# Attention in a hybrid block: one PSUM bank moved from the scores to the general pool, and half of the score products put behind the transposes of a query or key piece

## The chip, the cores and the metric

The kernel runs on one core of one Trainium2 chip. The metric is the time of one execution on the device in microseconds (us); lower is better. The kernel before the change took 1811.24 us, the median of three runs (1810.67 to 1813.12).

## What is computed

The reference is one hybrid block on x of shape 4 x 256 x 512 (four sequences of 256 positions, 512 channels), all in float32. Four residual steps follow each other, each on a layer norm of x: causal attention with 32 heads of 16 channels and an adapter of ten extra keys, a feed-forward with a selection of rows, a state space mixer (128 heads, by far the largest part), and the same feed-forward again. The change is in the attention:

```
q, k, v = split(x @ w_attn.T);  q, k = rope(q), rope(k)
scores  = q @ k.T / sqrt(16), causal
y       = softmax(scores) @ v
y      += gating * softmax(q @ ak.T / sqrt(512)) @ av     # ten adapter keys
out     = y @ w_proj.T
```

## The kernel before

The attention treats a sequence (b = 0 to 3) in eight units (u = 0 to 7) of four heads. This makes 32 iterations of the loop at line 705, numbered i = 8b + u. The stages of a unit are spread over several iterations, so that in iteration i the scores are of unit i, the transposes of the exponentials of unit i - 1, the product with the values of unit i - 2, and the gathering of unit i - 3. The inputs of later units and of the next sequence are made in the same iterations.

Everything that TensorE (PE) writes goes to PSUM, which has eight banks of 2 KB in each partition; every tile in question takes one bank. Three pools share them (lines 280 to 283): a_m with three banks, the general pool, whose tiles have the tag "m"; a_s with four banks for the scores (tag "sc"); and a_y with one bank for the product with the values. A tile that is asked for when all banks of its pool are taken gets the bank of an earlier tile, and its first writer waits until the readers of that earlier tile are done.

The order of PE's instructions is the order in which the code is written (manual_schedule at line 704). The instructions of the other engines are put in order by a planner that works with assumed costs. In one iteration PE does, in this order:

- **scores** (lines 475 to 510, a generator that yields twice). Eight products into four tiles: for c = 1 (the second 128 queries, against 256 keys) a pair of tiles of 2 x 256, then for c = 0 (the first 128 queries, against 128 keys) a pair of 2 x 128. Each tile takes two products (j = 0 and 1). Behind them VectorE (DVE) reads every tile twice at line 496 (it adds the mask, writes the sum to e and takes the maximum), eight reductions in all. Up to the first yield all this is issued; the second step issues the eight exponentials on ScalarE (ACT, line 505).
- **adapter_scores** (line 448, even iterations from 2 on): four products into "pa", copied to "sa" by ACT at line 456. Its second half transposes to "tra" later in the iteration, and ACT copies that to "as" at line 461.
- **pieces** (line 434): eight transposes into two tiles "trp" of a stack that POOL made, copied by ACT at line 444. They make a query or key piece for the scores of a later unit. Iterations 0 to 29 have them, 30 and 31 don't.
- the second step of **scores**, then the steps called "long" and "values": projections "pq" of the next sequence, output projections "po", the first products "pd" of the feed-forward (in iterations 30 and 31), all from groups of 512-wide or 288-wide products, and the adapter's product "pya", copied to "ya" by ACT at line 592.
- **weigh** (line 525): 16 products into "py", copied to "ys" by DVE at line 542.
- **turn** (line 512): twelve transposes into three tiles "ptr"; the first is copied to eT by ACT, the two others by DVE (line 522).
- **gathered** (line 545): two transposes of ys into "try", read by DVE at lines 553 and 554 (y).
- the rest of the adapter's scores, then the steps called "turn": the transposed norm "tr" (line 166; ACT and DVE copy it to axs at lines 107 and 108), "pt" (line 579) and "try" of line 605, which I call try2.

All of ptr, try, tra, trp, pa, tr, pt, pq, po, pd and pya are tiles of a_m. The pool a_s also holds the four projections of the first sequence before the loop (line 406).

In the loop the beginning of an iteration reads:

```
712  scoring = scores(b, u)
713  next(scoring)
...
721  if u % 2 == 0 and i > 0:
722      asides.append(adapter_scores(b, u // 2))
723      next(asides[-1])
724  if part:
725      next(part)
726  part = None
727  next(scoring)
728  step("long", i)
```

Of the kernel before, what the change touches and what calls it, by code (L numbers as in the profile page):

```python
# [79 lines left out]
def hybrid_kernel(  # L80
# [18 lines left out]
    a_s = keep.tile([P, 1], F32, name="a_s")  # L99
# [172 lines left out]
    def attention(later, region):  # L272
        with ExitStack() as es:
# [5 lines left out]
            p3 = pool("a3", 3)  # L279
            ps, ps_s, ps_y = (  # L280
                banks.enter_context(tc.tile_pool(name=name, bufs=bufs, space=PSUM))
                for name, bufs in (("a_m", 3), ("a_s", 4), ("a_y", 1))
            )

            acon = w1.tile([P, NCOL_ATTN - NCOL_KEEP], F32, name="acon")
# [181 lines left out]
            def begin(b):  # L467
                state[b] = {
                    "as": p1.tile([P, 2, NH, NA], F32, name="as"),
                    "y": p1.tile([P, 2, C], F32, name="y"),  # L470
                    "ya": p1.tile([P, 2, C], F32, name="ya", tag="ya"),
                    "yT": [p1.tile([P, KC, L], F32R, name=f"yT{j}") for j in range(2)],
                }

            def scores(b, u):

                qT, kT = turned_[b, u // 2]
                es_ = [p2.tile([P, 4, (c + 1) * P], F32, name=f"e{c}", tag=f"e{c}") for c in range(2)]
                made, tops = [], []
                for c in (1, 0):  # L480
                    n = (c + 1) * P

                    pair = [ps_s.tile([P, 2, n], F32, name="sc", tag="sc") for _ in range(2)]
                    for j in range(2):
                        blk = (u % 2) * 2 + j
                        for pr in range(2):
                            rows = slice(64 * pr, 64 * pr + 64)
                            nc.tensor.matmul(
                                pair[pr][:, j, :], qT[rows, blk, c * P : (c + 1) * P],
                                kT[rows, blk, :n], start=(j == 0), stop=(j == 1),  # L490
                            )
                    made += [(c, pr, sc) for pr, sc in enumerate(pair)]
                for c, pr, sc in made:
                    nm = p3.tile([P, 2], F32, name="nmx", tag="nmx", bufs=4)
                    for j in range(2):
                        nc.vector.tensor_tensor_reduce(  # L496
                            es_[c][:, 2 * j + pr, :].rearrange("p (k i) -> p k i", i=P),
                            sc[:, j, :].rearrange("p (k i) -> p k i", i=P), mask[:, 1 - c :, :],
                            -1.0, 3e38, ALU.add, ALU.min, nm[:, j : j + 1],
                        )  # L500
                    tops.append(nm)
                yield
                for (c, pr, sc), nm in zip(made, tops):
                    for j in range(2):
                        nc.scalar.activation(  # L505
                            es_[c][:, 2 * j + pr, :], es_[c][:, 2 * j + pr, :], AF.Exp, scale=-1.0,
                            bias=nm[:, j : j + 1],
                        )
                all_es[8 * b + u] = es_
                yield  # L510
# [120 lines left out]
            def fed(f, t):  # L631
                yield "turn", None
                xs = normed(f.norm, t)
                yield "long", max(0, B * 8 + t - 2)
                f.tile(t, xs, [ps.tile([P, FH], F32, name="pd", tag="m") for _ in range(2)])
# [41 lines left out]
            def moved(j, i):  # L677

                v = next(j, None)
                if v is None:  # L680
                    nexts.pop(j, None)
                else:
                    nexts[j] = v[0], i + 1 if v[1] is None else v[1]

            def step(stage, i):

                for j in [j for j, (s, r) in nexts.items() if s == stage and r <= i]:
                    moved(j, i)
# [15 lines left out]
            with tc.manual_schedule(engines={nc.tensor.engine}):  # L704
                for i in range(n):
                    b, u = divmod(i, 8)
                    if u == 0:
                        if i:
                            begin(b)
                        if b + 1 < B:  # L710
                            moved(prepared(b + 1), i)
                    scoring = scores(b, u)
                    next(scoring)
                    if i in FEEDS:
                        moved(fed(feed, FEEDS[i]), i - 1)
                    if i == 2:
                        nc.scalar.activation(a_s, a_s, AF.Exp)
                        nc.gpsimd.tensor_scalar(a_s, a_s, -1.0, None, ALU.mult)
                    if i == 3:
                        weights(wp_s, wproj, "ya", nc.gpsimd, p1)  # L720
                    if u % 2 == 0 and i > 0:
                        asides.append(adapter_scores(b, u // 2))
                        next(asides[-1])
                    if part:
                        next(part)
                    part = None
                    next(scoring)
                    step("long", i)
                    step("values", i)
                    if 2 <= i:  # L730
                        yss[i - 2] = weigh(*divmod(i - 2, 8), eTs.pop(i - 2))
                    if 1 <= i:
                        eTs[i - 1] = turn(all_es.pop(i - 1))
                    if 3 <= i:
                        gathered(*divmod(i - 3, 8), yss.pop(i - 3))
                    while asides:
                        next(asides.pop(0), 0)
                    step("turn", i)
                    if u == 7:
                        moved(adapted(b), i)  # L740
                    if 3 <= i:
                        if (i - 3) % 8 == 6:
                            moved(closed((i - 3) // 8, (0, 1, 2)), i)
                        if (i - 3) % 8 == 7:
                            moved(closed((i - 3) // 8, (3,)), i)

                    b, u = divmod(i + 3, 8)
                    if b < B:
                        part = pieces(b, u // 2, (i + 1) % 2)
                        next(part)  # L750
                    if i == 23:
                        inner.close()
                        feed = Feed("f", *(
                            later.enter_context(
                                tc.tile_pool(name=f"f{v}", bufs=v, side="right", reuse_waits="tile")
                            ) for v in (1, 2)
                        ))
                    if i in range(23, 27):
                        feed.weights(i - 23, nc.gpsimd)
                        feed.norm.stats(i - 23)  # L760
                    if i == 26:
                        feed.norm.root(0, 4)


                b = B - 1
                step("long", n)
                yss[n - 2] = weigh(b, 6, eTs.pop(n - 2))
                eTs[n - 1] = turn(all_es.pop(n - 1))
                gathered(b, 5, yss.pop(n - 3))
                step("turn", n)  # L770
                moved(fed(feed, 3), n - 1)
                step("turn", n)
                step("long", n + 1)
                step("values", n + 1)
                yss[n - 1] = weigh(b, 7, eTs.pop(n - 1))
                gathered(b, 6, yss.pop(n - 2))
                moved(closed(b, (0, 1, 2)), n)
                moved(fed(feed, 4), n)
                step("turn", n + 1)
                gathered(b, 7, yss.pop(n - 1))  # L780
                moved(closed(b, (3,)), n)
                step("long", n + 2)
                step("turn", n + 2)
                xs5 = normed(feed.norm, 5)
                assert not nexts, nexts
# [10 lines left out]
            with tc.tile_pool(name="f_c", bufs=5, space=PSUM, **freed) as ps_c:  # L796
# [22 lines left out]
                def products(t, j, cols=slice(0, FH)):  # L819
                    if (t, j) not in halves:  # L820
                        halves[t, j] = ps_c.tile([P, FH], F32, name="pd", tag="c")
                    feed.products(xss[t], j, halves[t, j], cols)
# [1010 lines left out]
    with ExitStack() as region:  # L1833
        mixer(*attention(later, region), later)
# [69 lines left out]
```

## Time and profile before

| What | Time |
|---|---|
| median of three runs | 1811.24 us |
| lowest and highest run | 1810.67, 1813.12 us |
| the profiled execution | 1812.82 us |
| its span, from the first to the last instruction | 1811.0 us |
| the stretch from 30 to 317 us, the attention loop | 287 us, PE busy 264.35, DVE 203.78, ACT 189.08, POOL 88.81 |
| from 317 to 400 us, the end of attention, the feed-forward and the start of the mixer | 83 us, PE busy 74.41, DVE 66.47 |
| from 400 us on, mostly the mixer | 1411 us, PE busy 1391.66 |
| TensorE clock granted, mean of the span | 0.994 |

The durations that the text works with come from the one profiled execution. All times inside it are counted from its first instruction. PE is TensorE with its products and transposes, PEld its loading of weights, DVE VectorE, ACT ScalarE, POOL GpSimd. A line such as "PE try L548 <- DVE eT L522: 3.2, 5, 1.1" says that PE, before instructions of line 548 that write the tile try, sat idle for 3.2 us in total, five times, at most 1.1 us, until instructions of DVE at line 522 that write eT had ended. In the timeline a row gives the start, the time taken, the engine, the line, the operation, the tiles (written <- read), the shapes and the number of instructions that were merged, and in brackets the idle time ahead of it and what ended it.

### The profile page before, as it was taken

What the parts mean: (1) busy time and instruction counts of PE and PEld (TensorE: products, weight loads), DVE (VectorE), ACT (ScalarE), POOL (GpSimd) and SP (SyncE); (2) the same over time, 40 slices, a digit from 0 to 9 for tenths busy, and PEclk for the clock granted to TensorE, in tenths of its full rate; (3) what the DMA queues carried; (4) which work ended last, traced back from release to release, by engine and by line L of the source; (5) the groups of instructions that cost most, each with busy time, mean ns of one, the idle gap of its engine ahead of it and who ended that gap; (6) DMA issues with size and microseconds to landing.
All of it is one profiled execution on the core that took longest, in us unless ns stands there. A gap on an engine that the chain in (4) does not pass through costs nothing.

```text
span 1811.0 us, 32937 instructions
## 1 busy us (share of the span) xinstructions
PE 1754.1 (97%) x12734; PEld 1425.0 (79%) x12734; DVE 1439.5 (79%) x2547; ACT 1268.4 (70%) x2289; POOL 250.9 (14%) x253
## 2 busy tenths in 40 slices
PE   8999988899999999999999999999999999999998
PEld 6777767778877888888888888888888888888877
DVE  6676677888998788878878797878787878887777
ACT  6666675487888667766866686768667866777754
POOL 6332230110110011011101111110111001101100
PEclk9999999999999999999999999999999999999999
DMA  4000000113243334423432343335323433343231
GB/s 151 1 1 1 23 15 26 43 59 106 94 134 125 105 94 135 134 76 103 162 109 93 94 146 99 100 94 170 99 93 104 154 105 94 111 140 112 85 98 57
DMA packets 134381, 169.51 MB, mean 94 GB/s; under 512 B 12240, under 2 KB 77520, under 8 KB 134224
## 3 DMA queue, kind: packets, MB, share of 16 engines
q1 hardware_dynamic: 125152, 134.37, 24.3%
q10 hardware_dynamic: 9072, 33.03, 4.8%
q8 instruction: 100, 1.64, 0.4%
q14 instruction: 57, 0.47, 0.1%
HBM read 131.71 MB, written 35.65 MB: 92 GB/s over the span
## 4 chain that ended last, share of the span: by engine, by line
PE 79%; DVE 10%; ACT 7%; issue 2%; POOL 1%; DMA 1%; SPq 0%; ACTq 0%; DVEq 0%; POOLq 0%
PE pp L115 14%; PE pp L117 13%; PE pp L116 13%; PE pyy L1244 8%; PE pog L115 6%; PE pog L116 6%; PE pog L117 6%; PE trx L1225 3%; PE ptr L521 1%; ACT e L505 1%; DVE acc L972 1%; PE pq L115 1%; PE pg L1162 1%; PE pq L116 1%; DVE eT L522 1%
## 5 line engine op out<-in xcount | busy, mean ns | idle before, releaser
L115 PE MATMUL pp<-mx,w 128*128 128x512 f32 x1144 | 459.3, 401 | 0.0
L117 PE MATMUL pp<-mx,w 128*128 128x512 f32 x1144 | 446.7, 391 | 0.0
L116 PE MATMUL pp<-mx,w 128*128 128x512 f32 x1144 | 446.1, 390 | 0.0
L1277 POOL TENSOR_TENSOR sq<-sq,x 128x1024 f32<-128x1024 f32 x54 | 132.1, 2446 | 1177.8 <-ACT x L1276 1177.8
L117 PEld LDWEIGHTS pp<-mx,w 128*128 128x128 f32 x1144 | 214.8, 188 | 46.2
L115 PEld LDWEIGHTS pp<-mx,w 128*128 128x128 f32 x1144 | 214.8, 188 | 44.6
L972 DVE SCALAR_TENSOR_TENSOR acc<-pp,cw_s,acc 128x1012 f32<-128x1012 f32 (+2 forms) x192 | 244.6, 1274 | 4.3
L116 PEld LDWEIGHTS pp<-mx,w 128*128 128x128 f32 x1144 | 215.2, 188 | 40.4
L1218 DVE TENSOR_TENSOR em<-em,gm 128x1280 f32<-128x1280 f32 x128 | 189.5, 1489 | 72.1 <-ACT em L1213 72.1
L115 PE MATMUL pog<-wo,gh 128*128 128x512 f32 x512 | 200.7, 392 | 1.9 <-DVE x L1373 1.9
L117 PE MATMUL pog<-wo,gh 128*128 128x512 f32 x512 | 199.7, 390 | 0.9 <-DVE gh L1356 0.9
L116 PE MATMUL pog<-wo,gh 128*128 128x512 f32 x512 | 199.4, 389 | 0.0
L1228 DVE TENSOR_TENSOR xd<-trx,dt_t 128x512 f32<-128x512 f32 x128 | 82.4, 686 | 141.4 <-PE trx L1225 141.4
L1144 ACT ACT_TABLE_LOAD x63 | 80.8, 1283 | 138.8 <-DVE acc L972 138.7
L1435 ACT ACTIVATE gt<-pp 128x1024 f32<-128x1024 f32 x64 | 65.6, 1025 | 145.2 <-PE pp L117 145.2
L1244 PEld LDWEIGHTS pyy<-em,xd 64*64 64x64 f32 x4096 | 130.2, 133 | 44.2 <-issue 17.3
L1205 ACT ACTIVATE em<-r,end_t 128x128 f32<-128x128 f32 x512 | 163.0, 389 | 0.8
L1244 PE MATMUL pyy<-em,xd 64*64 64x256 f32 (+3 forms) x4096 | 157.8, 300 | 3.1 <-DVE em L1218 2.9
L115 PEld LDWEIGHTS pog<-wo,gh 128*128 128x128 f32 x512 | 96.1, 188 | 24.7 <-issue 2.7
L117 PEld LDWEIGHTS pog<-wo,gh 128*128 128x128 f32 x512 | 96.1, 188 | 22.2 <-DVE gh L1356 2.1
L116 PEld LDWEIGHTS pog<-wo,gh 128*128 128x128 f32 x512 | 96.1, 188 | 19.4
L505 ACT ACTIVATE e<-e,nmx 128x256 f32<-128x256 f32 (+1 forms) x256 | 96.6, 450 | 19.9 <-DVE nmx L496 19.3
(323 smaller groups left out, 3131.8 us busy)
## 6 DMA issues: line engine op xcount, KB each, us to landing
wr<-in_win_dram SPq DMA_DIRECT2D x144, 256.0 KB, 2.8
r<-cumd SPq DMA_DIRECT2D x256, 128.0 KB, 2.9
spill<-gb ACTq DMA_DIRECT2D x63, 512.0 KB, 2.8
gr<-spill SPq DMA_DIRECT2D x120, 256.0 KB, 3.5
wor<-in_wout_dram SPq DMA_DIRECT2D x64, 256.0 KB, 4.5
out_dram<-x SPq DMA_DIRECT2D x7, 256.0 KB, 2.6
x<-in_x_dram SPq DMA_DIRECT2D x1, 1536.0 KB, 8.8
gr<-spill SPq DMA_DIRECT2D x8, 192.0 KB, 2.5
```

The costliest lines, as they stand in the source:

```text
L115: nc.tensor.matmul(o, lh, rh, start=(first and k == 0), stop=False)
L116: nc.tensor.matmul(o, lh, rl, start=False, stop=False)
L117: nc.tensor.matmul(o, ll, rh, start=False, stop=(last and k == n - 1))
L505: nc.scalar.activation(es_[c][:, 2 * j + pr, :], es_[c][:, 2 * j + pr, :], AF.Exp, scale=-1.0, bias=nm[:, j : j + 1],)
L972: nc.vector.scalar_tensor_tensor(av[:, :, d:], pv[:, :, : L - d], cw_s[:, ch, tap : tap + 1], av[:, :, d:], ALU.mult, ALU.add,)
L1144: nc.scalar.activation(pair(x2).rearrange("p k u i -> p u k i"), acc.rearrange("p (u k i) -> p u k i", u=2, i=Q), AF.Silu,)
L1205: nc.scalar.activation(piece(e, j, c, 2 - c, 2), rv[:, j, 2:, :], AF.Exp, bias=end_t[:, 2 * j + c, h : h + 1],)
L1218: nc.vector.tensor_tensor(e, e, gm, ALU.mult)
L1228: nc.vector.tensor_tensor(xd[:, hs, :].rearrange("p c (h d) -> p c h d", h=2), tr.rearrange("p c (h d) -> p c h d", h=2), dt_t[:, hs, 2 * ...
L1244: nc.tensor.matmul(py[d, u, j * L + c * Q : (j + 1) * L].rearrange("p (k i) -> p k i", i=Q), xd[us, 4 * j + c, d], piece(es2[hh], j, c)[us ...
L1277: (nc.gpsimd if n < NB - 2 else nc.vector).tensor_tensor(sqs[g], sqs[g], x2, ALU.add)
L1435: nc.scalar.activation(gts[i], pp, AF.Silu)
```

## The change

Three things change, all in the attention.

1. The pool a_m gets four banks instead of three, a_s three instead of four.
2. The generator of the scores yields three times instead of twice. Its first step now issues the four products of the second queries (c = 1) and their four reductions, its second step the four products of the first queries (c = 0) and their four reductions, and its third step the eight exponentials. The functions products and reduced hold the same instructions as before.
3. The loop calls the generator once more, behind the transposes of the piece. So on PE the adapter's four products and the eight transposes now stand between the products of the second and those of the first queries.

No instruction is added or taken away. The full diff:

```
-                for name, bufs in (("a_m", 3), ("a_s", 4), ("a_y", 1))
+                for name, bufs in (("a_m", 4), ("a_s", 3), ("a_y", 1))
...
                 made, tops = [], []
-                for c in (1, 0):
+
+                def products(c):
                     n = (c + 1) * P
-
                     pair = [ps_s.tile([P, 2, n], F32, name="sc", tag="sc") for _ in range(2)]
                     for j in range(2):
                         blk = (u % 2) * 2 + j
...
-                    made += [(c, pr, sc) for pr, sc in enumerate(pair)]
-                for c, pr, sc in made:
+                    for pr, sc in enumerate(pair):
+                        made.append((c, pr))
+                        reduced(c, pr, sc)
+
+                def reduced(c, pr, sc):
                     nm = p3.tile([P, 2], F32, name="nmx", tag="nmx", bufs=4)
                     for j in range(2):
                         nc.vector.tensor_tensor_reduce(
...
                     tops.append(nm)
-                yield
-                for (c, pr, sc), nm in zip(made, tops):
+
+                for c in (1, 0):
+                    products(c)
+                    yield
+                for (c, pr), nm in zip(made, tops):
                     for j in range(2):
                         nc.scalar.activation(
                             es_[c][:, 2 * j + pr, :], es_[c][:, 2 * j + pr, :], AF.Exp, scale=-1.0,
...
                     if part:
                         next(part)
                     part = None
+                    next(scoring)
                     next(scoring)
                     step("long", i)
                     step("values", i)
```

More of the change, by code (lines that the diff above doesn't have):

```diff
@@ L281, in attention @@
                 banks.enter_context(tc.tile_pool(name=name, bufs=bufs, space=PSUM))
-                for name, bufs in (("a_m", 3), ("a_s", 4), ("a_y", 1))
+                for name, bufs in (("a_m", 4), ("a_s", 3), ("a_y", 1))
             )
@@ L479, in scores, with products @@
                 made, tops = [], []
-                for c in (1, 0):
+                def products(c):
                     n = (c + 1) * P
@@ L491, in scores, with reduced @@
                             )
-                    made += [(c, pr, sc) for pr, sc in enumerate(pair)]
-                for c, pr, sc in made:
+                    for pr, sc in enumerate(pair):
+                        made.append((c, pr))
+                        reduced(c, pr, sc)
+                def reduced(c, pr, sc):
                     nm = p3.tile([P, 2], F32, name="nmx", tag="nmx", bufs=4)
@@ L501, in scores @@
                     tops.append(nm)
-                yield
-                for (c, pr, sc), nm in zip(made, tops):
+                for c in (1, 0):
+                    products(c)
+                    yield
+                for (c, pr), nm in zip(made, tops):
                     for j in range(2):
@@ L726, in attention @@
                     part = None
+                    next(scoring)
                     next(scoring)
```

## The prediction

> **What bounds the kernel now.** I read the page first: TensorE (PE) is busy 97% of the span and has 79% of the chain that ended last. Then the busy times by stage: the change touches only the attention loop, from about 30 to 300 us. Then the waits of PE in 24 to 320 us, and the timeline around them.
>
> ```profile
> PE 1754.1 (97%) x12734; PEld 1425.0 (79%) x12734; DVE 1439.5 (79%) x2547; ACT 1268.4 (70%) x2289; POOL 250.9 (14%) x253
> ...
> PEclk9999999999999999999999999999999999999999
> ```
> ```profile
> 107.00:166.00 59.00, 57.27 (x464) 44.53 (x460) 42.67 (x175) 37.99 (x94) 18.00 (x33) 1.00 0.01 2
> 166.00:175.00 9.00, 7.38 (x75) 5.74 (x74) 7.19 (x31) 6.55 (x16) 2.87 (x5) 1.00 0.00 0
> ...
> 231.00:252.00 21.00, 16.37 (x157) 12.95 (x158) 14.53 (x58) 17.12 (x39) 8.91 (x13) 0.93 0.04 13
> 252.00:283.00 31.00, 27.76 (x234) 20.87 (x233) 23.38 (x99) 21.26 (x54) 3.31 (x8) 0.93 0.01 2
> ```
> The columns are the stretch, its length, then busy time of PE, PEld, DVE, ACT and POOL, and the granted clock. Where an iteration holds a 512-wide product (107 to 166) PE is all but full. Where it holds none (166 to 175, and 231 to 283) PE is idle a tenth to a fifth of the time and waits for evictions:
>
> ```profile
> PE try L548 <- DVE eT L522: 3.2, 5, 1.1
> PE ptr L521 <- ACT ya L592: 2.2, 1, 2.2
> ...
> PE pq L115 <- ACT sa L456: 0.9, 2, 0.4
> ...
> PE tr L166 <- DVE eT L522: 0.8, 2, 0.4
> ```
> "try" does not read eT: it waits for a bank of the general pool a_m that the copy to eT still reads. Likewise ptr on ya, pq on sa, tr on eT. These are the waits a fourth bank can end.
>
> **What the change adds.** Scores of one iteration fill four tiles: two wide ones (second queries) and two narrow ones (first queries). With four banks in a_s nothing waits. With three, the second narrow tile reuses the bank of the first wide one, and has to wait until DVE has done both reductions of that tile. Iteration 13 shows whether the transposes cover this (PE, then DVE):
>
> ```profile
> 141.56 0.68 PE L488 MATMUL sc<-pc,pc 64*128 64x256 f32 x8
> 142.17 0.89 PE L442 MATMUL trp<-con,st 128*128 128x128 f32 x8
> 142.90 0.50 PE L115 MATMUL pq<-wv,axs 128*128 128x512 f32 x1
> ```
> ```profile
> 142.21 0.42 DVE L496 CUSTOM_DVE_ANT_0 e<-sc,acon 128x256 f32<-128x256 f32 x1 [0.28 <-PE sc L488]
> ...
> 142.56 0.28 DVE L554 TENSOR_TENSOR y<-try,ry 128x128 f32<-128x128 f32 x1
> 142.76 0.41 DVE L496 CUSTOM_DVE_ANT_0 e<-sc,acon 128x256 f32<-128x256 f32 x1
> ```
> They do not. The four wide products take 0.34 us (start of the fifth product less start of the first, in the trace), the eight transposes 0.73 (142.17 to 142.90), so after the change PE wants that bank at about 141.56 + 0.34 + 0.73 + 0.07 = 142.70. The second reduction ends at 142.76 + 0.41 = 143.17. A semaphore takes about 0.06 (an eT copy that ends at 141.22 lets tra start at 141.28), and three narrow products behind it 0.20 (three times 0.068, from four in 0.27). So pq starts at second end + 0.26 = 143.43 and not at 142.90: **0.53 us lost**, all on PE's path, since 12 products queue behind in order and the rotation on DVE, the copies on ACT and the next transposes wait for them. In even iterations four adapter products (0.53) stand between as well: in iteration 4 the second reduction ends 1.61 after the first score product, so 1.87 is wanted, and pq starts at 1.93 anyway. No wait there, only one more change from transposes to 64-row products. No row shows this change alone; between nothing and the 0.17 us that PEld idles ahead of score weights now, I take 0.07, what trp costs more behind adapter products than behind scores (0.80 against 0.73).
>
> The same sum for every iteration, with the end of the second reduction and the present start of what follows on PE, both counted from the first score product, and the loss (end + 0.26 - start):
> 0: 2.36, 2.05, 0.57. 1: 1.46, 1.47, 0.25. 3: 2.02, 1.83, 0.45. 5: 1.73, 1.45, 0.54. 7, 13, 15, 21, 23: 1.61, 1.34, 0.53 each. 9 and 17: 2.02, 1.74, 0.54 each. 10: 2.13, 1.95, 0.44. 11 and 19: 1.84, 1.34, 0.76 each. 18: 1.90, 2.07, 0.09. 25: 1.42, 1.59, 0.09. 27: 1.84, 1.80, 0.30. 29: 2.36, 2.18, 0.44. Sum 8.4.
> The nine even ones without a wait (2, 4, 6, 12, 14, 20, 22, 26, 28): 0.07 each, 0.6.
> 8, 16, 24: 0.52, 1.06, 1.10, where DVE's softmax sums of the adapter come first. I count nothing: there ptr is followed by a wait for DVE (1.0 us at 171.57) that begins only when the last reduction ends, and the late ptr hides in it.
> 30 and 31 have no transposes between (the pieces are used up): 2.35 against 1.15, 1.46; 2.10 against 0.61, 1.75. Behind them ptr, tr and try now wait 0.77 + 0.38 and 0.75 for banks, which the fourth bank frees, so 0.3 and 1.0 remain: 1.3.
> **Cost 8.4 + 0.6 + 1.3 = 10.3 us.** The narrow reductions themselves do not come late: DVE works on the wide ones until 2.30 after the start, and their tiles are there by about 2.1. No DMA and nothing on POOL is moved; reductions pass only copies that are ACT's.
>
> **What the change removes.** Waits of PE for a bank of a_m, from its timeline. Left out are those that end in data (POOL's stacks, y, axs) and those already in the starts above or used up at 30 and 31. First the wait, then what I count:
> First iterations, 41.90 to 44.02 (0.62, 0.39, 0.21) and 52.03 (0.68): 1.9, all, since the bank then comes from a tile copied long before. 60.41: 0.2, all.
> tr at 116.19 and 183.76 (0.41 each), try2 at 125.10 and 192.79 (0.38), tr at 274.32 (0.38): 2.0, all.
> pq or po behind sa at 135.62, 203.31, 267.92 (0.44, 0.43, 0.53): 0.31, 0.31 and 0.5, together 1.1, since the scores' bank is next at the first two (pq 2.07 after the first score product and not 2.38).
> The groups behind 8, 16 and 24 (1.4, 1.6, 1.4): 1.1, as the reductions set the pace and the late ptr eats the rest.
> try at 234.52: 1.06, all; its data, ys, was there at 232.99.
> ptr at 249.24 (2.19): 0.9. Its second tile gets a bank that was free at 244.5, the third still waits for ya behind eight exponentials; eight transposes took 1.76 there, half of it moves into the wait.
> try, tra and try2 at 256.56 to 264.95 (1.0): 0.7. pt at 306.18 and 307.45 (1.0): 0.7.
> **Gain 9.6 of 15.1 listed.** The lower end is a third of the list, 5.0 (each wait moves on to the next tile, as at ptr); the upper all of it. I take each by the data behind it, as said.
>
> **Sum.** +10.3 - 9.6 = +0.7 us. The profiled execution took 1812.82 us (span 1811.0 and 1.8 around it), so 1813.5 for it; it lies 1.6 above the median of the runs, 1811.24, and against that the forecast is **1811.9**.
>
> **The clock.** The rows show it at half in short stretches: granted 0.93 over 231 to 252 and again over 252 to 283. At 259.50 the eight transposes take 1.15 to the next product instead of 0.73, and the py group 1.44 instead of 0.79; with ptr's 1.91 for 1.53 that is about 1.4 us a stretch. It followed waits of only 0.35, 0.16 and 0.53. So a stretch more or fewer is 1.4 either way, and I take none. The Trainium skill, TensorE: Matmul & The Clock Gate, "What's actually happening", halves the clock after an idle window of about 3.4 us; by it the new waits, of half a microsecond to two, would never slow PE, and the sum would stay. This trace has it sooner. The same page, Part 4, says that transposes don't count as busy as products do, which fits 256 to 260, nearly all transposes.
>
> **Rivals.**
> The fourth bank wins. All 15.1 come back and 30 and 31 hide whole: 15.1 - 9.0 = 6.1 faster, **1805.1**. For it: the last eight iterations have few wide products, and PE waits most there. Against it: in 8 and 16 DVE's reductions, not a bank, hold the next step.
> The scores' wait is not hidden in 8, 16, 24, 30 and 31. This is the slower side: PE comes late to ptr there, and DVE waits for PE instead. Price 2.7 for the three and 1.9 for the two: +5.3, **1816.5**. It decides from the point where ptr's second tile comes after DVE would start to copy it: in iteration 16 that is 4.04 (ptr, now 2.98, plus 1.06) + 1.1 = 5.14 after the first score product against 4.79, so it is near.
> The fourth bank doesn't do what it says: tiles wait for the next slow copy, only a third is gained: 10.3 - 5.0, again +5.3, 1816.5. Against it: the waits at 116, 183 and 234 have their data ready.
> If DVE takes the two wide reductions without y between them (0.20), the new waits shrink by 0.2 in some 15 iterations, 3.0 less; that is inside the range.
>
> **Chances.** Forecast 0.44, fourth bank wins 0.24, wait not hidden 0.24, bank of no use 0.08. This kernel can be told from no change by about 0.2%, 3.6 us. The forecast's own range is that of no change, 1807.6 to 1814.9; the others are one faster, two slower: 0.24, 0.44, 0.32. The bounds of the terms (cost 6 to 15, gain 5 to 15) and two stretches of clock reach from 1804.5 to 1819.5.
>
> **What would show it.** Right: sc of four and four, the second four starting about 0.5 us after trp in odd iterations, waiting for DVE L496; trp starting 0.27 sooner after the wide scores; no wait of tr, try or pq on eT or sa at iterations 10, 11, 12. Wrong: no wait ahead of the narrow scores, or ptr waiting there for L496; and a changed number of half-clock stretches would add what the sum leaves out.

## The result, and the profile after

| | median | lowest to highest | runs |
|---|---|---|---|
| before | 1811.47 us | 1810.67 to 1813.12 | 4 |
| after | 1820.62 us | 1819.47 to 1821.81 | 4 |

The ratio is 1.0044, with a 95% interval of 1.0031 to 1.0057: the change makes the kernel slower, by 5.6 to 10.3 us. The forecast was 1811.9 us and no difference, with a range of its own from 1807.6 to 1814.9 us. The profiled execution of the changed kernel took 1819.51 us, with a span of 1817.7 us.

The page of the changed kernel, busy times and granted clock:

```profile
PE 1765.8 (97%) x12734; PEld 1438.1 (79%) x12734; DVE 1439.4 (79%) x2547; ACT 1269.1 (70%) x2289; POOL 250.4 (14%) x253
...
PEclk8999999999999999999999999999999999999999
```

PE has the same 12,734 instructions and is busy 11.7 us longer. An instruction also counts as busy while it runs at half clock or stands behind another, so this alone names no cause. The same four stretches as before (stretch, its length, busy PE, PEld, DVE, ACT, POOL, granted clock):

```profile
107.00:166.00 59.00, 56.82 (x441) 45.08 (x439) 40.37 (x171) 37.16 (x92) 16.72 (x32) 1.00 0.01 2
166.00:175.00 9.00, 8.48 (x87) 6.65 (x85) 7.60 (x30) 6.44 (x17) 4.22 (x6) 1.00 0.00 0
231.00:252.00 21.00, 19.61 (x166) 15.00 (x158) 17.16 (x65) 15.60 (x35) 12.21 (x17) 0.92 0.11 30
252.00:283.00 31.00, 27.27 (x233) 21.34 (x233) 22.82 (x98) 24.33 (x60) 4.17 (x11) 0.94 0.00 1
```

Where the iteration holds 512-wide products (107 to 166), PE now starts 441 instructions in 59 us, where it started 464 before. (The same times hold slightly earlier work in the changed kernel, whose iteration 13 begins at 144.14 and not at 141.56, so these rows give an impression and no sum.) The view of what PE waited for, 24 to 330 us of the changed kernel (total us, times, longest):

```profile
PE sc L488 <- DVE nmx L499: 12.5, 22, 1.9
...
PE ptr L527 <- DVE eT L528: 0.8, 1, 0.8
PE try L554 <- DVE eT L528: 0.8, 1, 0.8
...
PE tra L460 <- ACT eT L528: 0.4, 1, 0.4
...
PE tr L166 <- ACT paT L589: 0.2, 1, 0.2
PE try L611 <- ACT eT L528: 0.2, 1, 0.2
```

The waits on eT, sa, ya and as that stood in the view of before (13.9 us in all) are down to 2.2 (the four lines here that end in eT). The fourth bank does its work. In their place stands one line that was not there: the products of the scores wait 22 times for DVE's reductions, 12.5 us. The following table shows that this line understates them. It splits the time from the first score product of iteration 0 to the start of the last pya product, 32 iterations, into two sums of start times on PE: from the first score product of each iteration to the first product behind scores, adapter products and the piece's transposes (the score piece), and all the rest. The last three kernels are experiments told below.

| kernel | score piece | rest | together |
|---|---|---|---|
| before | 59.6 | 224.3 | 283.9 |
| after | 81.0 (+21.4) | 209.4 (-14.9) | 290.5 (+6.5) |
| split alone | 67.6 (+8.0) | 222.3 (-2.0) | 289.9 (+5.9) |
| four general banks shared with py, scores unsplit | 52.4 (-7.2) | 212.6 (-11.7) | 265.0 (-19.0) |
| the same, scores split | 61.3 (+1.7) | 212.1 (-12.2) | 273.4 (-10.5) |

From before to after the rest gives back 14.9 us, and the score piece takes 21.4. Outside this part the spans differ by 0.2 us. Iteration 13 of the changed kernel shows the piece, PE first, then DVE:

```profile
144.14 0.50 PE L488 MATMUL sc<-pc,pc 64*128 64x256 f32 x4
144.58 0.89 PE L442 MATMUL trp<-con,st 128*128 128x128 f32 x8
145.39 0.32 PE L488 MATMUL sc<-pc,pc 64*128 64x128 f32 x1
145.91 0.41 PE L488 MATMUL sc<-pc,pc 64*128 64x128 f32 x3 [0.19 <-DVE nmx L499]
146.25 0.50 PE L115 MATMUL pq<-wv,axs 128*128 128x512 f32 x1
```
```profile
144.79 0.42 DVE L499 CUSTOM_DVE_ANT_0 e<-sc,acon 128x256 f32<-128x256 f32 x1
145.14 0.08 DVE L499 DVE_READ_ACCUMULATOR2_ANT nmx<- 128x1 f32 x1
145.14 0.29 DVE L560 TENSOR_TENSOR y<-try,ry 128x128 f32<-128x128 f32 x1
145.34 0.41 DVE L499 CUSTOM_DVE_ANT_0 e<-sc,acon 128x256 f32<-128x256 f32 x1
145.68 0.08 DVE L499 DVE_READ_ACCUMULATOR2_ANT nmx<- 128x1 f32 x1
```

The second narrow product waits, as forecast, for both reductions of the first wide tile; the read of their accumulator, which the forecast did not have, ends at 145.76. pq then starts 2.10 us after the first score product; before it was 1.34. That is 0.77 (with the unrounded starts) and not 0.53. The bracket says 0.19: it counts idle time only from the modelled end of the product ahead, 145.39 + 0.32. But nothing keeps the second narrow product from starting with the first: in the split kernel with four score banks it starts 0.003 or 0.004 us after it in all 32 iterations. Here it starts 0.52 us after it.

Read in this way, the products wait in 31 of the 32 iterations (all but iteration 2), from 0.15 to 2.16 us and 21.7 us in all, where the view shows 22 waits and 12.5 us. In iteration 4, where the forecast saw no wait, the second narrow product starts 0.15 us after the first, and the row has no bracket; the four take 0.56 us and not the 0.44 that they take where nothing holds them:

```profile
71.70 0.56 PE L488 MATMUL sc<-pc,pc 64*128 64x128 f32 x4
72.19 0.50 PE L115 MATMUL pq<-wq,axs 128*128 128x512 f32 x1
```

### The profile page after: what moved, and what is told of

It reads as the page before. It is cut to its first block, busy times and chain, and to the rows that moved or that the text cites. A ratio compares the mean times of both kernels' runs of the same rounds, so it can differ in the third digit from the quotient of the medians.

```text
span 1817.7 us, 32954 instructions
## 1 busy us (share of the span) xinstructions
PE 1765.8 (97%) x12734; PEld 1438.1 (79%) x12734; DVE 1439.4 (79%) x2547; ACT 1269.1 (70%) x2289; POOL 250.4 (14%) x253
## 4 chain that ended last, share of the span: by engine, by line
PE 78%; DVE 11%; ACT 6%; issue 2%; POOL 1%; DMA 1%; ACTq 0%; SPq 0%; DVEq 0%; POOLq 0%
PE pp L115 12%; PE pp L117 12%; PE pp L116 12%; PE pyy L1251 7%; PE pog L115 6%; PE pog L116 6%; PE pog L117 6%; PE trx L1232 3%; PE ptr L527 2%; DVE acc L979 2%; ACT em L1212 1%; PE pq L115 1%; DVE em L1225 1%; PE sc L488 1%; PE pq L116 1%
## 5 line engine op out<-in xcount | busy, mean ns | idle before, releaser
L919 DVE TENSOR_TENSOR w<-wr,w 128x512 fp32r<-128x512 f32 x138 | 99.7, 727 | 4.4 <-ACT w L916 4.4
```

Of the source, the lines that this page charges most:

```text
L919: nc.vector.tensor_tensor(w[1], r, w[0].bitcast(F32), ALU.subtract)
```

## The experiments

The theory at the start of the experiments: the split has a price of its own, the narrow products' wait comes on top, and the fourth bank gives back about what the list of waits says. The rival: the fourth bank does nothing, and the wait is the whole cost.

**Split alone** (three general banks, four for scores; the generator and the loop as in the change):

```diff
-                for name, bufs in (("a_m", 4), ("a_s", 3), ("a_y", 1))
+                for name, bufs in (("a_m", 3), ("a_s", 4), ("a_y", 1))
```


> The split of the scores with the banks as before (three general, four for scores). Theory: the loss has three terms, the wait for the scores' third bank (12.5 us of PE idle in the changed kernel), a fixed price of taking the four wide and four narrow products apart (about 0.2 us an iteration, 6 us in all: 0.61 us for eight together; apart, the four wide ones take 0.44, the change to 64-row products 0.09 more, the narrow ones 0.27), and more half-clock stretches. Here the first is gone and the 15 us of waits for the general pool remain: some 6 us over before, about 1817.5, and no wait of PE at L488 on the reductions. Rival, that the split is nearly free and the wait is all (the prediction had 0.07 us in nine iterations): within 2 us of before, 1811 to 1813.

Measured: 1820.19 us, ratio to before 1.0043 (1.0026 to 1.0060). The split alone, without any wait for a scores' bank, costs about as much as the whole change. The median is above what either side expected, but the interval (4.7 to 10.9 us) holds the theory's 6. Iterations 13 and 6 in its timeline of PE:

```profile
148.10 0.51 PE L488 MATMUL sc<-pc,pc 64*128 64x256 f32 x4
148.64 0.84 PE L442 MATMUL trp<-con,st 128*128 128x128 f32 x8
149.41 0.44 PE L488 MATMUL sc<-pc,pc 64*128 64x128 f32 x4
149.78 0.50 PE L115 MATMUL pq<-wv,axs 128*128 128x512 f32 x1
```
```profile
88.39 0.50 PE L488 MATMUL sc<-pc,pc 64*128 64x256 f32 x4
88.82 0.70 PE L452 MATMUL pa<-pc,akbd 128*80 128x256 f32 x4
89.36 0.46 PE L442 MATMUL trp<-con,st 128*128 128x128 f32 x4
90.07 0.51 PE L442 MATMUL trp<-con,st 128*128 128x128 f32 x4 [0.25 <-ACT sa L456]
90.51 0.44 PE L488 MATMUL sc<-pc,pc 64*128 64x128 f32 x4
90.88 0.50 PE L115 MATMUL pq<-wv,axs 128*128 128x512 f32 x1
```

Nothing is idle in iteration 13 by the brackets, and pq still comes 1.68 after the first score product, 0.34 later than before. Four wide products alone take 0.43 (iteration 6) or 0.54 us until the next product starts, four narrow ones 0.37 until pq, together 0.80 to 0.91; all eight in one go took 0.61. In iteration 6 the second transposes also wait 0.25 for a bank; such waits of trp, ended by ACT at sa, come seven times in this kernel (1.9 us). The view of before has none for trp, and neither has that of the split kernel with four general banks below, so they belong to the split with three.

**Banks alone** (four and three, the scores not split; the second step of the generator follows the first at once):

```diff
-                for name, bufs in (("a_m", 3), ("a_s", 4), ("a_y", 1))
+                for name, bufs in (("a_m", 4), ("a_s", 3), ("a_y", 1))
```


> Four general banks and three for scores, with the narrow products directly behind the wide ones as before. Theory: the wait for the third bank is then no longer covered by transposes and adapter products; the second reduction ends about 1.6 to 2.4 us after the first product, the narrow ones want the bank at 0.4: some 1.4 us in each of 32 iterations, 45 us, less about 15 us of waits for the general pool and less what hides in light iterations: 1835 to 1845. Rival, that the wait hides behind other waits: no slower than the changed kernel, 1820.

Measured: 1867.27 us, ratio 1.0301 (1.0281 to 1.0321). Its waits of PE:

```profile
PE sc L488 <- DVE nmx L499: 43.3, 29, 2.2
```

The theory expected 45 us of this wait and 1835 to 1845 us in all. The view's 43.3 fits only in appearance: by the starts, the second narrow products wait 1.1 to 2.4 us in each iteration, 55.0 us together. The score piece is 51.0 us longer than before (110.6 us), and the rest, which was to give back some 15, is 3.5 longer too. From the first score product to the last pya product 78.5 us run at half clock, 17.1 in before; what share of the time that makes was not tried. So the split is what makes three score banks bearable at all: it leaves 21.7 of 55 us of waiting, at a price.

**py in the general pool, scores as before** (no bank of its own for py; four and four):

```diff
-                for name, bufs in (("a_m", 3), ("a_s", 4), ("a_y", 1))
+                for name, bufs in (("a_m", 4), ("a_s", 4))
...
-                py = ps_y.tile([P, L], F32, name="py", tag="py")
+                py = ps.tile([P, L], F32, name="py", tag="m")
```


> The kernel before with four banks in the general pool and four for the scores; the product py has no bank of its own and takes one of the general pool. Scores as before, not split. Theory: the waits for the general pool (15 us listed before, 2.4 left in the changed kernel) go with no price: 1798 to 1803. Rival, that such a wait only moves to the next tile or engine (the prediction counted 9.6 of 15.1 and py takes a bank): 1805 to 1811.

Measured: 1796.24 us, ratio 0.9919 (0.9900 to 0.9939). A fourth general bank is worth 11 to 18 us if it is taken from py and not from the scores; the median lies a little under the theory's 1798 to 1803. This is the fastest of all kernels here, faster than before and after.

**Narrow scores first** (the changed kernel, with the first queries' products ahead of the transposes and the second queries' behind):

```diff
-                for c in (1, 0):
+                for c in (0, 1):
```


> The changed kernel with the pairs in the other order: the narrow products (first queries) ahead of the transposes, the wide ones behind. The bank is then released by two narrow reductions (0.28 us each instead of 0.42). Theory: the release comes 0.3 to 0.4 us sooner, the 12.5 us of waiting fall to about 4, the fixed price stays: 1810 to 1814. Rival, that the half-clock stretches and not the wait make the loss: 1818 to 1821 as the changed kernel.

Measured: 1813.3 us, ratio 1.0003 (0.9993 to 1.0014). The time is as expected, the wait isn't: 9.0 us in 15 waits. By the starts of the products the wait is 17.5 us, where the changed kernel has 21.7. That the tile with the short reductions is freed sooner does shorten the waits, by 4 us, but the time fell by 7. The mean granted clock of the twelve runs is 0.9933, that of the changed kernel's four 0.9898, so the rival (the half-clock stretches) may have a part in it. The time therefore doesn't confirm the reason.

**Split with shared py**, to settle whether the split's price hangs on the banks:

```diff
-                for name, bufs in (("a_m", 4), ("a_s", 3), ("a_y", 1))
+                for name, bufs in (("a_m", 4), ("a_s", 4))
...
-                py = ps_y.tile([P, L], F32, name="py", tag="py")
+                py = ps.tile([P, L], F32, name="py", tag="m")
```


> Here the general pool has four banks (the py tiles among them), the scores have four, and the scores are split as in the changed kernel, so no score product should wait for a bank. The theory says that the split has a fixed price, about 8 us, which the split alone showed with no wait for a scores' bank, and that it is paid whatever the pools are: 1796.2 us of the unsplit kernel with the same banks plus 8 = about 1804 us (1801 to 1807). The rival says that the price of the split alone came from the split work meeting three general banks (its trace shows 1.9 us of trp waits on sa that were not there before): then it goes with four general banks, and the time is 1796 to 1799 us.

Measured: 1804.51 us, ratio 0.9960 (0.9948 to 0.9973); the rival, 1796 to 1799, falls. Iteration 13 of the unsplit kernel with these banks, then of this one:

```profile
134.03 0.68 PE L488 MATMUL sc<-pc,pc 64*128 64x256 f32 x8
134.64 0.89 PE L442 MATMUL trp<-con,st 128*128 128x128 f32 x8
135.36 0.46 PE L115 MATMUL pq<-wv,axs 128*128 128x512 f32 x1
```
```profile
140.08 0.50 PE L488 MATMUL sc<-pc,pc 64*128 64x256 f32 x4
140.52 0.88 PE L442 MATMUL trp<-con,st 128*128 128x128 f32 x8
141.32 0.44 PE L488 MATMUL sc<-pc,pc 64*128 64x128 f32 x4
141.69 0.50 PE L115 MATMUL pq<-wv,axs 128*128 128x512 f32 x1
```

1.33 us became 1.61, with no wait in either. The same difference, 0.26 to 0.32, stands in 17 of the 21 iterations from 3 to 23; the other four (8, 10, 16, 18) lie between -0.14 and 0.22. These 17 make 4.9 of the 9.0 us by which the two score pieces of the table differ; iterations 25 and 26 make 2.0 more.

**Three banks shared by the general pool and py**, one bank idle (against the kernel with shared py, scores unsplit):

```diff
-                for name, bufs in (("a_m", 4), ("a_s", 4))
+                for name, bufs in (("a_m", 3), ("a_s", 4))
```


> Here py shares the general pool as in the fast kernel, but that pool has three banks and one bank lies idle; scores unsplit, four banks. The theory says that the fourth general bank is what gained there, and that giving py a place in a pool of three takes a bank away from the others now and then: no faster than before, 1812 to 1822 us. The rival says that it was py that gained, since it no longer waits for its one bank: then this kernel is about as fast as the one with four shared banks, 1796 to 1802 us.

Measured: 1819.92 us, ratio 1.0040 (1.0027 to 1.0052). So it is the fourth bank that gains, not py's sharing. The waits of PE are many and small:

```profile
PE ptr L521 <- ACT eT L522: 2.0, 6, 0.4
PE ptr L521 <- DVE ys L542: 1.9, 5, 0.5
...
PE tra L460 <- ACT eT L522: 1.5, 2, 0.8
```

ptr reads neither eT nor ys; it waits for their banks.

**Second products and exponentials behind the step "long"** (against the changed kernel):

```diff
+                    step("long", i)
                     next(scoring)
                     next(scoring)
-                    step("long", i)
```


> The changed kernel with the second four products, and the exponentials, behind the step called long instead of ahead of it. The theory says that the products then find their bank free (the 12.5 us of waits fall to 2 or less), while the fixed price of the split, about 8 us, and the gain of the fourth general bank, about 15 us, stay: 1820 - 11 = about 1808 us (1804 to 1812). The rival says that the later reductions and exponentials are late for the transposes of the next iteration, so that the wait comes back there as a wait for the exponentials: 1815 us or more.

Measured: 1812.03 us, ratio 1.0002 (0.9993 to 1.0012), the upper end of the theory's range. Both sides were partly right:

```profile
PE tra L460 <- ACT eT L528: 4.6, 8, 0.8
PE sc L488 <- DVE nmx L499: 3.4, 5, 1.0
...
PE pa L452 <- ACT eT L528: 2.0, 3, 1.5
PE try L611 <- ACT eT L528: 1.5, 3, 0.7
```

The wait for the scores' banks falls from 12.5 to 3.4 (by the starts of the products from 21.7 to 4.5), and the waits for ACT's copies to eT, 0.6 in the changed kernel, come to 8.1 in the lines shown. That ACT copies late since its exponentials now come behind "long" is argued from the order, not tried.

**Five general banks** (py among them, three for scores, narrow first):

```diff
-                for name, bufs in (("a_m", 4), ("a_s", 3), ("a_y", 1))
+                for name, bufs in (("a_m", 5), ("a_s", 3))
...
-                for c in (1, 0):
+                for c in (0, 1):
...
-                py = ps_y.tile([P, L], F32, name="py", tag="py")
+                py = ps.tile([P, L], F32, name="py", tag="m")
```


> Scores split with the narrow ones first, three banks for them, and five for the general pool with py among them. The theory says that a fifth general bank finds nothing left to gain, that the split costs its 8 us, and that the wait for a scores' bank stays at about 9 us: 1796 + 8 + 9 = 1813, less what such waits let the other engines catch up, so 1807 to 1814 us. The rival says that general banks are still short at four: then 1798 to 1804 us.

Measured: 1813.54 us, ratio 1.0006 (0.9998 to 1.0014). With 9.2 us of waits for the scores' banks and the same median it is like the narrow-first kernel with four and one (1813.3): in the time, a fifth place, shared with py, brings nothing. The two profiled runs don't settle it. The loop, measured as in the table, is 280.7 us here and 287.6 there, but that profile is of the slowest of its runs (1816.41), with 23.9 us of the loop at half clock and not 17.1, and behind the loop this kernel takes about 3 us longer.

## Where the prediction was right and where it was wrong, point by point

The path between before and after can now be walked in three measured steps, each by the difference of the ratios to before, times 1811.5 us: before to shared py with four banks, -14.7; to the split, +7.4; to three score banks with py back in its own, +15.2. Together +8.0.

The sign of the forecast's +0.7 us came true, but that is luck: it was what remained of two terms of about ten, and the forecast itself called it no difference. All four runs of the changed kernel lie above the range that it gave for itself. The outer reach of 1804.5 to 1819.5 does not follow from its own bounds either: cost 6 to 15, gain 5 to 15 and two stretches of clock at 1.4 reach from about 1799 to 1824.

- **What bounds the kernel, and the mechanism of the new wait: right.** Four and four products, a wait for the reduction (L499 in the changed kernel), and no wait on eT or sa in iterations 10 to 12.
- **"So pq starts at second end + 0.26": the step that failed; it is + 0.49.** Its parts were 0.06 for the semaphore and 0.20 for three narrow products. In iteration 13 the second reduction ends at 145.75, the second narrow product starts 0.16 later (the read of the accumulator lies between), and pq 0.34 after that (146.245 less 145.910). Together it is 0.49 or 0.50 in 27 of the 32 iterations. In the 18 iterations of the forecast's list the later start of what follows sums to 14.8 us, where 8.4 was forecast. 18 times 0.23 is 4.1 of the missing 6.4; the next point is most of the rest.
- **"The end of the second reduction as before": also wrong in places.** In iterations 11 and 19 it comes 2.41 and 2.40 after the first score product, not 1.84, and in 27 2.39 and not 1.84. The split alone doesn't do this: in iterations 11 and 19 of the kernel with the split alone it is 1.84, with the split and four shared banks 2.39, and with four shared banks and no split 2.17. In 19 DVE still adds y of L605 (0.61 us at 198.31) just ahead of the reductions, where before it was through with that sum earlier. That PE, with the fourth bank, reaches the scores earlier against DVE is read from these rows; no run shows it by itself.
- **"No wait" in the nine even iterations, and "one more change from transposes to 64-row products, 0.07": wrong.** There is a wait in eight of the nine. In 4, 6, 14 and 22 the second narrow product starts 0.15 us after the first, and the piece is 0.24 or 0.25 us longer: with 0.49 for 0.26, pq can't start before 1.61 + 0.49 = 2.10 after the first score product, and it started at 1.93 before (2.18 now, since the reduction ends at 1.69). The price of the change itself shows where no bank is waited for, between the two kernels with shared py: about 0.29 an iteration. It was looked for in one place, and the cost is in two: ahead of the transposes (0.44 and not 0.34 until trp starts) and behind them. trp came 0.17 sooner in iteration 13 (0.44 for 0.61), not 0.27. In the changed kernel this price is not paid on top of the wait: what starts behind the wait is set by the reduction's end.
- **8, 16, 24, 30 and 31: right in three of five.** Their later starts sum to 6.6 us, where 2.7 + 3.2 was forecast before anything was taken off. At iteration 16 py comes 0.68 later, the 1.01 us wait of try behind ptr is gone, and the iteration is shorter (7.89 for 8.23), as 8 is (7.35 for 8.34) and 30 (8.80 for 9.18). Iteration 24 is longer (9.14 for 7.15): its later start is 2.18 and not 1.10, and a stretch of half clock begins in it at 244.3. From the first score product of iteration 31 to the last pya product it is 1.6 longer, where 1.0 was forecast, again with a stretch of half clock in it (at 302.3). The rival that put all five on the slower side named the right sign and, three times in five, the wrong place.
- **Gain 9.6, and what 8, 16, 24, 30 and 31 hide: about right, a little low.** 9.6 + 2.7 + 1.9 = 14.2 was forecast, of which 1.8 (the waits at 52.03, 135.62, 203.31 and 267.92) lies in the score piece and 12.4 in the rest; the rest gave back 14.9. The rival "bank of no use" is refuted by the kernels with four and with three shared banks (1796.24 and 1819.92 us). "The fourth bank wins" had the gain, and lost by the same mis-sized cost.
- **The clock, of which nothing was counted: a part of the result, at most half, its size not shown.** From the first score product to the last pya product before has 17.1 us at half clock, after 23.9, two stretches more. That can cost 3.4 us at most (half of 6.8), or 2.8 by the prediction's 1.4 a stretch, of the 6.5 us by which this part is longer. In the whole span it is 22.4 and 37.4 us, but outside this part the spans differ by 0.2 us. The kernel with the split alone has 17.1 us as before has, and is 5.9 us longer in this part, so the split costs time without more half clock. The changed kernel's four runs have mean clocks of 0.989 to 0.991, the profiled run of before 0.994. In 40 runs of the kernel before, beside the experiments, the clock lies between 0.991 and 0.997, and the time falls by 1.09 us for each 0.001 (correlation -0.91); that the two go together doesn't say how much of this change is clock. The wait in iteration 19 of the changed kernel is followed by such a stretch (windows of the time ahead of it and of the stretch itself; the eighth column is the clock):

```profile
196.48:199.89 3.41, 2.42 (x22) 1.78 (x20) 3.19 (x14) 2.71 (x8) 1.49 (x4) 1.00 0.00 0
199.89:203.31 3.42, 3.42 (x10) 2.67 (x11) 1.25 (x12) 2.34 (x7) 0.22 (x1) 0.50 0.02 5
```
```profile
198.44 0.33 PE L488 MATMUL sc<-pc,pc 64*128 64x128 f32 x1
199.75 0.52 PE L488 MATMUL sc<-pc,pc 64*128 64x128 f32 x3 [0.99 <-DVE nmx L499]
200.20 0.80 PE L115 MATMUL pq<-wq,axs 128*128 128x512 f32 x1
```

PE is idle for only 0.99 us of the 3.41 ahead by this view, among transposes and scores, and the next 3.42 run at 0.50. The Trainium skill, TensorE: Matmul & The Clock Gate, "What's actually happening", asks for a whole idle window; these rows differ, and the measurement decides. Which waits bring a stretch and which don't stays open: the wait of 0.98 at 130.22 brought none.

Adding up for the profiled runs: the score piece +21.4, where 13.1 was forecast (8.4 + 0.6 + 2.7 + 3.2 less the 1.8 of gain that lies in it); the rest -14.9, where 12.4 was; outside 0.2. That is +6.7 us of span, where +0.7 was forecast. The cost is 8.3 over, the gain 2.5 over, and the gap of 6.0 is their difference: 6.4 of the 8.3 lie in the 18 iterations of the list, 1.2 in the nine even ones and 0.7 in the other five. The half-clock time is inside these sums, not on top of them.

## What to carry to other kernels

Price a split of a run of small products by what stands on both sides of each half, and take the price from start times: a run that is cut in two loses its overlap twice, with no wait in any view. A bank that is freed by a reduction is late by the whole chain behind it (accumulator read, release, the rest of the products, the change to the next shape; 0.49 us here), and the reduction itself can move against PE when another edit frees PE elsewhere. A wait that no bracket shows can be read from the starts of products that belong together. Before a bank is taken from a pool, ask which pool can spare it: here py could and the scores could not.

## What the runs showed of the hardware

- Eight 64-row products in one run take 0.61 us to the next start; as four and four between 128-row work they take 0.44 and 0.37. The two changes cost 0.2 us more and the transposes between them 0.08 more (0.80 for 0.72 in the two fences of iteration 13 with shared py).
- The view of waits showed 12.5 us in 22 places, the start times 21.7 us in 31 iterations. A first product that stands alone counts as busy for 0.32 us, though its follower starts 0.003 or 0.004 us after it where no bank is waited for.
- From the end of a DVE reduction whose accumulator is then read (0.08 us) to the start of the product that takes over its bank 0.15 to 0.16 us pass in 31 of the 32 iterations.
- The granted clock differs between runs of one kernel (0.991 to 0.997 in 40 runs), and a mean of 0.001 less goes with 1.09 us more in this one. A comparison below 0.3% should list the clocks.
